# One attention and feed-forward stack on one core: the softmax steps of a unit planned closer together, its joins later, x loaded two tiles ahead, the weight check's end cut in three

## The chip, the cores and the metric

The kernel runs on one core of one Trainium2 chip. The metric is the device time of one execution in microseconds (us). Three runs of the kernel before took 2451.07, 2451.25 and 2455.77 us, so the median is 2451.25 us. One further execution was profiled. It took 2450.27 us, and its instructions span 2448.4 us of that.

Engines are named as the profile names them. PE is the matrix engine and PEld its weight load. DVE is the vector engine, ACT the scalar engine, POOL the general-purpose engine. SP has no arithmetic here and issues transfers. A trailing q (SPq, ACTq) marks the part of an engine that issues and waits. Each engine takes its instructions strictly in the order in which the program lists them for it.

## What is computed

Inputs are float32; x has 64 batches of 64 rows and 1024 columns. Cut to what matters:

```python
def reference(x, cond, lang, ...):
    y = einsum('bct,bcd->bdt', x, weights[cond])        # one 64x64 matrix chosen per batch
    qkv = y @ qkvw + qkvb                               # 32 heads of 32
    probs = softmax((q @ k.T) / sqrt(32))               # 64 x 64 per batch and head
    x = x + (probs @ v) @ ow + ob
    base = x @ W.T                                      # plus a low-rank part that top-2 gates mix
    z = base + 2.0 * lora(x, gates(x, lang))
    q, s = dynamic_quant(z * inv)                       # rounded to -127..127
    inter = clip(silu(q_g @ w_gate.T * ...) * (q_u @ w_up.T * ...), -10, 10)
    return x + dynamic_quant(inter * inv_inter) @ w_down.T * ...
```

## The kernel before

The 4096 rows are cut into 8 blocks of 512 (a block has four tiles of 128 rows, PB = 4). The first stage (function `attention`) makes queries, keys, values, softmax and context. The second makes the output projection (`OutProjection`) and the feed-forward part. Large products are done as seven smaller ones (the table `Winograd.ORDER` is 1, 6, 7, 5, 2, 4, 3); four of the operand quarters' sums are made beforehand.

**The order is written out by a planner.** `attention` is one Python loop that emits instructions for all engines. It keeps a plan time `now` and a heap `due`. `at(time, f)` puts a step into the heap. `run` (line 674) first emits every step whose time has come, then one PE product (a "fill"), then the evacuation ("rest") of the product before it, and moves `now` on by the fill's cost: 1.72 for a query or key product, 3.43 for a value product or an output product. So plan times are not waited for on the chip. They only decide the order of the instructions on each engine, and each engine then runs as fast as its order and its waits let it.

A block has four phases c = 0 to 3, one for each pair of head groups. A phase's fills are the products for the next phase: 7 for q and 7 for k, about 24 us; in phases 0 and 3 there are 7 for v as well, about 48 us. In every phase `group` emits the scores of one pair of head groups (128 small matmuls into the four PSUM banks of the pool `ps_s`, which has one buffer) and handles four units, n = 0 to 3, each 128 x 512 probabilities:

- `exponents` (L559, L560 on DVE, L564 on ACT): maximum, difference, exponential;
- `normalize` (L570 to L572 on DVE): sum, reciprocal, product;
- `parted` (L578 on ACT): a copy `ph` that lays the two 16-bit halves of each float apart; two buffers;
- `turned` (L583 on SP): a DMA transpose of `ph` into `phT`; two buffers;
- `joined` (L590 on ACT): a copy that puts the halves together again, `pT`; four buffers.

The start of unit n is planned 2.7 us after that of unit n - 1. At plan time 13.7 of the next phase `contexts` multiplies the four `pT` with the values (L603), and ACT copies the result out (`co`, L615) and stores it. Both the results of `contexts` and those of the conditional tile (below) stand in the same single `ps_s` buffer, so the next scores or the next conditional tile waits until ACT has read it.

**Conditional tiles.** `conditional_tile` makes y for one tile: 8 small matmuls (L393) that read `x` and the gathered matrix `wg`, then two copies `yh` on ACT (L404), two DMA transposes `yhT` on SP (L412) and copies into place on POOL (L426). Right after its matmuls the next tile's rows are loaded (`load_x`, L243) into the one buffer that `x` has, and POOL gathers its `wg` (L245). Most phases have one such tile. Phase 0 of block 0 has three, at plan times 13.7, 25 and 37.

**Weights.** In block 0 the weights come from the inputs, DVE or POOL makes the sums, and POOL stores the seven quarters (L291 for q and k, L311 for v). Later blocks load them ready (L293, L297). The load of a q or k job is issued when the job two places earlier has done its last product. The load of a value quarter is issued when the product that used its buffer is done; in block 0 it waits for the store of that buffer too.

**Chores.** `halve_weights` casts the feed-forward weights to bfloat16 in 24 steps and compares. It is a generator, and the planner takes one step of it at a time (two to four in a phase). Its end finds the maximum over all comparisons: a reduction on DVE, a store of one column, a load of it as a row, and a reduction of that row (L135 to L142). `combine_quarters` follows it.

In the last phase (block 7, c = 3) the fills are the first two pairs of the output projection, 14 products of 3.43. Each pair's results are also transposed: `xh` on ACT (L1198), `xhT` on SP (L1200), `xTo` on ACT (L1209), a store on SP (L1210). Then `out_dram` is stored and the next pair's `cx` and `xo` are loaded on SP (L1250, L1179, L1185).

Of the kernel before, what the change touches and what calls it, by code (L numbers as in the profile page):

```python
# [96 lines left out]
def halve_weights(tc, st, const, dram, srcs, half, any_i):  # L97


    nc = tc.nc  # L100
    parts = []
    for nm, (src, k, n) in srcs.items():
        v = src.rearrange("(k p) n -> p k n", p=P)
        parts += [(nm, v, i, slice(c, c + 512)) for i in range(k) for c in range(0, n, 512)]
    other = const.tile([P, len(parts)], F32, tag="other", name="other")
    tiles = {}

    def load(u):
        if u < len(parts):
            _, v, i, cols = parts[u]  # L110
            tiles[u] = st.tile([P, 512], F32, tag="t", name=f"hw_{u}")
            nc.sync.dma_start(tiles[u], v[:, i, cols])

    copied = None

    def compared():
        if copied:
            u, t, b = copied
            nc.vector.tensor_tensor(t, t, b, ALU.not_equal)
            nc.vector.tensor_reduce(other[:, u:u + 1], t, AX.X, ALU.max)  # L120

    load(0)
    for u, (nm, v, i, cols) in enumerate(parts):
        yield
        compared()
        load(u + 1)
        t = tiles.pop(u)
        b = st.tile([P, 512], BF16, tag="b", name=f"hb_{u}")
        nc.gpsimd.tensor_copy(b, t)
        nc.gpsimd.dma_start(half[nm][:, i, cols], b)  # L130
        copied = (u, t, b)
    yield
    compared()
    seen = st.tile([P, 1], F32, tag="seen", name="seen")
    nc.vector.tensor_reduce(seen, other, AX.X, ALU.max)  # L135
    seen_d = dram.tile([P, 1], F32, tag="seen_d", name="seen_d")
    nc.sync.dma_start(seen_d, seen)
    row = st.tile([1, P], F32, tag="row", name="row")
    nc.sync.dma_start(row, seen_d.rearrange("p o -> o p"))
    any_f = st.tile([1, 1], F32, tag="any_f", name="any_f")  # L140
    nc.vector.tensor_reduce(any_f, row, AX.X, ALU.max)
    nc.vector.tensor_copy(any_i, any_f)  # L142
    yield
# [39 lines left out]
def attention(tc, a, x_t, ctx_d, ident, dram, ps_g, KC, PB, NBLK, NCH, HPC, H, C, chores, early, op):  # L183
# [27 lines left out]
    with ExitStack() as ctx, ExitStack() as mid:  # L211
# [25 lines left out]

        def load_x(b, j, pool_=xp, tag="x"):
            i = b * PB + j
            xt = pool_.tile([P, H], F32, tag=tag, name=f"x_{i}")  # L240
            if i == PB - 1:
                held(xt[:, 0:1], x_of[0, 0][0])
            nc.sync.dma_start(xt, x_t[i])  # L243
            wg = xp.tile([P, C], F32, tag="wg", name=f"wg_{i}", bufs=4)
            nc.gpsimd.indirect_dma_start(  # L245
                out=wg[:, :],
                out_offset=None,
                in_=cw,
                in_offset=bass.IndirectOffsetOnAxis(ap=idx[:, i:i + 1], axis=0),
            )  # L250
            x_of[b, j] = xt, wg
# [130 lines left out]
        def conditional_tile(b, j, banks=None):  # L382

            xt, wg = x_of.pop((b, j))
            Y = Ys[b]
            if banks is None:
                banks = ps_s.tile([P, 4, 512], F32, tag="s", name=f"cond_{b}_{j}")
            ps = [banks[:, 2 + hf, :] for hf in range(2)]  # L390
            for hf in range(2):
                for r in range(2):
                    nc.tensor.matmul(  # L393
                        ps[hf][halves[r ^ hf], :], wg[halves[r], :], xt[halves[r], hf * 512:(hf + 1) * 512],
                        start=True, stop=True,
                    )
            if j + 1 < PB:
                load_x(b, j + 1)
            elif b + 1 < NBLK:
                load_x(b + 1, 0)  # L400

            def parted_y(hf):
                h = w.tile([P, 2, 512], I16, tag="yh", name=f"yh_{b}_{j}_{hf}", bufs=2)
                nc.scalar.copy(h, planes(ps[hf]))  # L404
                hs[hf] = h

            hs, hTs = {}, {}

            def turned_y(hf):
                h = hs[hf]  # L410
                hT = w.tile([P, 2, 512], I16, tag="yhT", name=f"yhT_{b}_{j}_{hf}", bufs=2)
                nc.sync.dma_start(  # L412
                    hT.rearrange("p h (k q) -> p (h k) q", q=P), h.rearrange("p h t -> p (h t)"), transpose=True
                )
                hTs[hf] = hT

            def joined_y(hf):
                key = f"B{hf + 1}{j // 2 + 1}"
                if j % 2 == 0:
                    Y[key] = quarter_of(b, key)  # L420
                src = hTs[hf].rearrange("p h (k q) -> p h k q", q=P)
                for r in range(2) if hf else (slice(0, P),):
                    q = halves[r ^ hf] if hf else r
                    q = slice((j % 2) * P + q.start, (j % 2) * P + q.stop)
                    dst = Y[key].bitcast(I16).rearrange("p k (q h) -> p h k q", h=2)[:, :, :, q]
                    nc.gpsimd.tensor_copy(dst, src[:, :, :, halves[r] if hf else r])  # L426

            for time, f, hf in (
                (1.7, parted_y, 0), (3.4, parted_y, 1), (3.5, turned_y, 0), (5.1, turned_y, 1), (8.5, joined_y, 0),
                (10.2, joined_y, 1),  # L430
            ):
                at(now + time, lambda f=f, hf=hf: f(hf))
# [213 lines left out]
        def group(b, c):  # L646


            def begin():
                ps = scores(b, c)  # L650
                pTs = []
                waiting.append((b, c, pTs))
                for n in range(NU):
                    at(now + 2.7 * n, lambda n=n: first(n, ps, pTs))

            def first(n, ps, pTs):
                p = exponents(b, c, n, ps)
                at(now + 10.8, lambda: normalize(b, c, n, p))
                at(now + 13.5, lambda: second(n, p, pTs))

            def second(n, p, pTs):
                h = parted(b, c, n, p)
                at(now + 1.7, lambda: third(n, turned(b, c, n, h), pTs))

            def third(n, hT, pTs):
                at(now + 6.8, lambda: fourth(n, hT, pTs))

            def fourth(n, hT, pTs):
                pTs.append(joined(b, c, n, hT))
                if (b, c) == (NBLK - 1, NP - 1) and len(pTs) == NU:  # L670
                    at(now + 3.4, contexts)
            return begin
# [76 lines left out]
        for b in range(NBLK):  # L749
            if b == 0:  # L750
                load_x(1, 0)
            for c in range(NP):
                fills, length = [], None
                if c + 1 < NP:
                    fills += qk_fill(b, c + 1)
                    if c == 0:
                        fills[7:7] = v_fill(b, 1)
                        if b == 0:
                            for at_ in range(3, 7):
                                with_sums(fills, at_, v_raw, 1)  # L760
                        if b == 0:
                            at(now + 25, lambda: conditional_tile(1, 1))
                            at(now + 37, lambda: conditional_tile(1, 2))
                    if c + 2 == NP and b + 1 < NBLK:
                        sums_to_come = [lambda b=b, n=n: t_of(b + 1, Ys[b + 1], *T_OF[n]) for n in range(4)]
                        with_sums(fills, -2, sums_to_come, 1)
                        with_sums(fills, -1, sums_to_come, 1)
                elif b + 1 < NBLK:

                    assert len(Ys[b + 1]) == 6  # L770
                    fills += v_fill(b + 1, 0) + qk_fill(b + 1, 0)
                    with_sums(fills, 0, sums_to_come, 1)
                    with_sums(fills, 1, sums_to_come, 1)
                    B = Ys[b + 1]
                else:
                    behind.pop()()
                    mid.close()
                    op.open_rest()
                    fills += op.pair(0) + op.pair(1)
                    length = 24  # L780
                if b + 1 == NBLK and c == 1:
                    assert next(chores, None) is None
                    early.close()
                    for n, load in enumerate(op.open_weights()):
                        at(now + 5 * n, load)
                phase(b, c, fills, length or sum(f[0] for f in fills))
# [1020 lines left out]
```

## Time and profile before

| what | us |
|---|---|
| median of three runs | 2451.25 |
| the profiled execution | 2450.27 |
| its span | 2448.4 |
| PE busy in the span | 2383.1 |
| DVE / ACT / POOL busy | 1358.8 / 939.4 / 432.6 |
| PE idle in 0 to 20 (start of the kernel) | 9.15 |
| PE idle in 2400 to 2448.4 (end of the kernel) | 16.3 |
| first scores from / last context to | 69.0 / 1411.3 |
| mean granted PE clock | 0.991 |

The profile has a page (busy times, 40 slices, queues, a chain of waits, groups of instructions) and can be asked for more: who waited for whom, all instructions of a stretch in order of time (the timeline), and busy times and granted clock by stretches. In a line of the waits stand the waiting instruction, what ended its wait, the total in us, how often, and the longest. In a line of the timeline stand the start, the length, the engine, the line, the operation with output and inputs, how many were merged, and in brackets the idle time before it with what ended it.

### The profile page before, as it was taken

Reading aid. Unit: us, or ns where it says so; the run is one execution under the profiler, and the core shown is the slowest. Engines: PE = TensorE matmul, PEld = TensorE weight load, DVE = VectorE, ACT = ScalarE, POOL = GpSimd, SP = SyncE. Lnnn points to the kernel's source line nnn. Section 1 sums busy time; section 2 is a strip of 40 time slices with the busy share of each in tenths; the row PEclk is TensorE's granted clock in tenths of the full one; section 3 lists DMA queues with packets and bytes.
Section 4 is the critical chain, followed back from the end, with each engine's and each line's share of the span. In section 5 each row is a group of like instructions: output and inputs, shape, how many; then the busy total and the mean of one; then the engine's idle time right before and its main releaser. Section 6 shows DMA issues by size and latency. Waiting matters only on the chain.

```text
span 2448.4 us, 41643 instructions
## 1 busy us (share of the span) xinstructions
PE 2383.1 (97%) x17104; PEld 1631.7 (67%) x17104; DVE 1358.8 (55%) x2584; ACT 939.4 (38%) x1220; POOL 432.6 (18%) x476
## 2 busy tenths in 40 slices
PE   8899999999999999999999999999999999999997
PEld 7778888888788888878888444444454545445453
DVE  3465465474463453643644632433367777878787
ACT  1235343353353343533533544344423333333333
POOL 4121121121232232310000333433200000000000
PEclk9999999999999999999999999999999999999999
DMA  8798687796797897866757768886744443434343
GB/s 291 246 272 217 194 245 207 227 253 191 212 259 214 237 251 226 242 191 195 203 150 231 211 211 261 260 252 203 237 135 82 87 80 80 87 69 92 76 115 78
DMA packets 478729, 463.23 MB, mean 189 GB/s; under 512 B 359874, under 2 KB 414147, under 8 KB 464835
## 3 DMA queue, kind: packets, MB, share of 16 engines
q1 hardware_dynamic: 448018, 393.90, 57.7%
q0 software_dynamic: 12080, 49.82, 7.8%
q10 hardware_dynamic: 18432, 16.79, 2.4%
q8 instruction: 136, 2.23, 0.4%
q14 instruction: 63, 0.51, 0.1%
HBM read 274.02 MB, written 100.66 MB: 153 GB/s over the span
## 4 chain that ended last, share of the span: by engine, by line
PE 86%; DMA 5%; ACT 3%; SPq 2%; DVE 2%; issue 1%; ACTq 0%; DVEq 0%
PE poc L1103 4%; PE pskc L491 4%; PE pskd L491 4%; PE pod L1103 4%; PE pbc L1103 4%; PE pba L1103 4%; PE pbd L1103 4%; PE poa L1103 4%; PE pska L491 4%; PE psqa L491 4%; PE psqd L491 4%; PE psqc L491 4%; PE psva L512 3%; PE psvc L512 3%; DMA phT<-ph 3%; PE psvd L512 3%
## 5 line engine op out<-in xcount | busy, mean ns | idle before, releaser
L578 ACT COPY ph<-prob 128x1024 int16<-128x1024 int16 x128 | 133.7, 1045 | 226.3 <-DMA phT<-ph 157.4
L590 ACT COPY pT<-phT 128x1024 int16<-128x1024 int16 x128 | 168.1, 1337 | 87.4 <-DMA phT<-ph 87.2
L564 ACT ACTIVATE prob<-prob 128x512 f32<-128x512 f32 x128 | 80.4, 628 | 255.0 <-DVE prob L560 254.4
L426 POOL COPY yB<-yhT 128x512 int16<-128x512 int16 (+1 forms) x84 | 86.8, 1085 | 496.8 <-DMA yhT<-yh 481.4
L1610 POOL DMA_DIRECT2D out_dram<-y x29 | 25.0, 862 | 656.3 <-DVE y L1602 644.2
L559 DVE TENSOR_REDUCE mx<-s 128x8 f32<-128x512 f32 x128 | 87.4, 683 | 75.1 <-PE s L550 75.1
L1224 POOL TENSOR_TENSOR xo<-xo,ob 128x1024 f32<-128x1024 f32 x32 | 84.9, 2672 | 221.3 <-DMA xo<-in_x_dram 213.5
L491 PE MATMUL psqa<-yB,wq 128*128 128x256 f32 x512 | 121.3, 379 | 1.3 <-ACT psqp L461 0.7
L1198 ACT COPY xh<-xo 128x1024 int16<-128x1024 int16 x64 | 64.2, 1040 | 149.8 <-DVE xo L1243 149.3
L491 PE MATMUL pska<-yB,wk 128*128 128x256 f32 x512 | 121.1, 379 | 0.2 <-ACT pskp L461 0.2
L512 PE MATMUL psva<-wv,yB 128*128 128x256 f32 x512 | 119.3, 387 | 0.0
L1103 PE MATMUL poa<-woA,cx 128*128 128x512 f32 x256 | 115.2, 593 | 0.0
L512 PEld LDWEIGHTS psva<-wv,yB 128*128 128x128 f32 x512 | 98.6, 194 | 20.9 <-issue 5.7
L1103 PE MATMUL pba<-wtA,x1T 128*128 128x512 f32 x240 | 107.9, 592 | 0.0
L491 PEld LDWEIGHTS psqa<-yB,wq 128*128 128x128 f32 x512 | 97.0, 190 | 15.4 <-ACT psqp L461 1.5
L1209 ACT COPY xTo<-xhT 128x1024 int16<-128x1024 int16 x64 | 84.8, 1338 | 58.3 <-DMA xhT<-xh 51.6
L491 PEld LDWEIGHTS pska<-yB,wk 128*128 128x128 f32 x512 | 97.2, 190 | 13.7 <-ACT pskp L461 0.6
L615 ACT ACTIVATE co<-banks,bqkv 128x256 f32<-128x256 f32 x124 | 59.0, 475 | 121.9 <-PE banks L393 89.9
L1240 POOL TENSOR_TENSOR xo<-xo,ou 128x512 f32<-128x512 f32 x48 | 59.5, 1267 | 210.4 <-DVE ou L1237 210.4
L572 DVE TENSOR_TENSOR prob<-prob,den 128x512 f32<-128x512 f32 x128 | 93.5, 730 | 4.4
L560 DVE TENSOR_TENSOR prob<-s,mx 128x512 f32<-128x512 f32 x128 | 88.5, 691 | 6.1
L1103 PEld LDWEIGHTS poa<-woA,cx 128*128 128x128 f32 x256 | 48.6, 190 | 60.4 <-issue 60.0
(258 smaller groups left out, 4978.1 us busy)
## 6 DMA issues: line engine op xcount, KB each, us to landing
wv<-v_d SPq DMA_DIRECT2D x98, 512.0 KB, 4.9
wq<-q_d SPq DMA_DIRECT2D x28, 1792.0 KB, 7.9
wk<-k_d SPq DMA_DIRECT2D x28, 1792.0 KB, 8.6
x<-in_x_dram SPq DMA_DIRECT2D x32, 512.0 KB, 5.4
ctx_d<-co ACTq DMA_DIRECT2D x128, 128.0 KB, 4.7
cx<-ctx_d SPq DMA_DIRECT2D x16, 1024.0 KB, 6.9
xo<-in_x_dram SPq DMA_DIRECT2D x32, 512.0 KB, 5.5
xT_d<-xTo SPq DMA_DIRECT2D x64, 256.0 KB, 2.8
```

The costliest lines, as they stand in the source:

```text
L426: nc.gpsimd.tensor_copy(dst, src[:, :, :, halves[r] if hf else r])
L491: nc.tensor.matmul(ps[:, 0:HB], A[:, SLOT[A_OF[i]], k, :], B[B_OF[i]][:, k, :], start=first and k == 0, stop=k == KQ - 1, skip_group_check ...
L512: nc.tensor.matmul(ps[:, j * VC:(j + 1) * VC], B[B_OF[i]][:, k, j * P:(j + 1) * P], A[:, k, :], start=first and j == 0 and k == 0, stop=k ...
L559: nc.vector.tensor_reduce(mx, ps[:, :, n, :, :], AX.X, ALU.max)
L560: nc.vector.tensor_tensor(p.rearrange("p j h k -> p h j k"), ps[:, :, n, :, :], mx.unsqueeze(3).to_broadcast([P, HPC, 2, C]), ALU.subtract,)
L564: nc.scalar.activation(p, p, AF.Exp, scale=scale)
L572: nc.vector.tensor_tensor(p, p, den.unsqueeze(2).to_broadcast([P, n, C]), ALU.mult)
L578: nc.scalar.copy(h, planes(p.rearrange("p n k -> p (n k)")))
L590: nc.scalar.copy(planes(pT.rearrange("p a b q -> p (a b q)")), hT)
L1103: self.nc.tensor.matmul(ps, self.B[self.B_OF[i]][:, k, :], self.A[self.A_OF[i]][:, k, :], start=first and k == 0, stop=k == self.KQ - 1, s ...
L1209: nc.scalar.copy(planes(xT.rearrange("p k q -> p (k q)")), hT)
L1224: nc.gpsimd.tensor_add(s["x"][:, t, :], s["x"][:, t, :], self.ob)
```

## The change

Four constants and three small pieces of code change:

- `normalize` of a unit is planned 4.0 after its exponents (was 10.8), `parted` 5.4 after (was 13.5), `turned` still 1.7 after that, and `joined` 10.3 after the transpose (was 6.8);
- `x` has two buffers in its pool, and each conditional tile loads the tile two ahead; two tiles are loaded before phase 0 of block 0;
- `halve_weights` gives way to the planner after the store of the column and after the load of the row.

```diff
@@ halve_weights
     seen_d = dram.tile([P, 1], F32, tag="seen_d", name="seen_d")
     nc.sync.dma_start(seen_d, seen)
+    yield
     row = st.tile([1, P], F32, tag="row", name="row")
     nc.sync.dma_start(row, seen_d.rearrange("p o -> o p"))
+    yield
     any_f = st.tile([1, 1], F32, tag="any_f", name="any_f")
     nc.vector.tensor_reduce(any_f, row, AX.X, ALU.max)
@@ load_x
-            xt = pool_.tile([P, H], F32, tag=tag, name=f"x_{i}")
+            xt = pool_.tile([P, H], F32, tag=tag, name=f"x_{i}", bufs=2 if tag == "x" else None)
@@ conditional_tile
-            if j + 1 < PB:
-                load_x(b, j + 1)
-            elif b + 1 < NBLK:
-                load_x(b + 1, 0)
+            if PB * b + j + 2 < PB * NBLK:
+                load_x(*divmod(PB * b + j + 2, PB))
@@ group
             def first(n, ps, pTs):
                 p = exponents(b, c, n, ps)
-                at(now + 10.8, lambda: normalize(b, c, n, p))
-                at(now + 13.5, lambda: second(n, p, pTs))
+                at(now + 4.0, lambda: normalize(b, c, n, p))
+                at(now + 5.4, lambda: second(n, p, pTs))
...
             def third(n, hT, pTs):
-                at(now + 6.8, lambda: fourth(n, hT, pTs))
+                at(now + 10.3, lambda: fourth(n, hT, pTs))
@@ attention, the loop over blocks
             if b == 0:
                 load_x(1, 0)
+                load_x(1, 1)
```

## The prediction

> **What bounds the kernel.** I read the busy times first, then the waits of PE, then the waits of SP, then the timeline around each long wait of PE.
>
> ```profile
> PE 2383.1 (97%) x17104; PEld 1631.7 (67%) x17104; DVE 1358.8 (55%) x2584; ACT 939.4 (38%) x1220; POOL 432.6 (18%) x476
> ...
> PE pskb L491 <- ACT qT L474: 8.3, 6, 1.9
> PE banks_None_None L603 <- ACT pT L590: 7.0, 2, 6.5
> PE cond L393 <- DMA x<-in_x_dram: 6.3, 1, 6.3
> PE psvc L512 <- DVE psvu L464: 5.3, 1, 5.3
> ```
>
> PE is busy for 2383 of 2448 us, so only its idle time can be won. The start and the end of the kernel, 25 us of it, are not touched. What is left is this short list, and each edit aims at one line: the weight check at 5.3, the x loads at 6.3, the softmax plan at 8.3 and 7.0. A long wait also costs clock: the window 600 to 620 has a granted clock of 0.92, and the 16 matmuls after the wait of 5.26 took 5.65 us where such sixteen elsewhere show 3.62.
>
> ```profile
> SPq L583 <- ACT pT L590: 116.1, 25, 7.2
> ...
> SPq L297 <- DMA v_d<-wv: 10.1, 1, 10.1
> ```
>
> These two waits of SP speak against the change. The first says that a transpose already waits for a join: `phT` has two buffers, so unit 2's transpose cannot go before unit 0's join is done, and everything behind it on SP stands still. The second says that in block 0 a value load held SP for 10.1 us.
>
> I followed the planner's rule for both plans to get each engine's order. In a 24 us phase the old order is transposes 0, 1, join 0, transpose 2, 3, join 1, 2, 3. The new one is all four transposes and then four joins. SP will thus stop at transpose 2 until join 0 and at transpose 3 until join 1, in every phase.
>
> **Weight check.**
>
> ```profile
> 601.07 0.38 SPq L137 DMA_DIRECT2D seen_d<-seen  x1
> ...
> 611.14 0.29 SPq L139 DMA_DIRECT2D row<-seen_d  x1
> ...
> 613.47 0.28 DVE L141 TENSOR_REDUCE any_f<-row 1x1 f32<-1x128 f32 x1 [15.16 <-DMA row<-seen_d]
> ...
> 619.85 5.65 PE L512 MATMUL psvc<-wv,yB 128*128 128x256 f32 x16 [5.26 <-DVE psvu L464]
> ```
>
> DVE stands 15.16 us for two trips to memory in a row. SP too stands 10 us, between 601.07 and 611.14. With two more yields the row load comes some 20 plan us after the store, and the reduction one chore (3.4 plan us) after the load, which landed 2.33 us after its issue (611.14 to 613.47). So DVE waits at most about 1 us, and PE's PSUM slack covers that. Won: 5.26 + (5.65 - 3.62) = **7.3 us**. Bounds 5 to 7.3. The chores needed rise by two, which pushes `combine_quarters` back by two chores; the plan has more than ten free chores before its results are read, so that costs nothing; without them the program would not build.
>
> **Rows of x.** The wait is 6.28 us, the cold matmuls after it 1.98 against 1.09 and 5.66 against 3.62. If it simply went, 9.2 us would be won. But I ask what is late next.
>
> ```profile
> 86.16 1.06 POOL L311 DMA_DIRECT2D v_d<-wv  x2
> ...
> 93.43 0.34 SPq L297 DMA_DIRECT2D wv<-v_d  x1
> 93.89 1.18 SPq L243 DMA_DIRECT2D x<-in_x_dram  x1
> ...
> 96.42 3.05 SPq L583 DMA_TRANSPOSE phT<-ph  x1
> ...
> 102.49 1.98 PE L393 MATMUL cond<-x,wg 64*64 64x512 f32 x8 [6.28 <-DMA x<-in_x_dram]
> ...
> 104.78 1.04 ACT L578 COPY ph<-prob 128x1024 int16<-128x1024 int16 x1 [12.71 <-DMA phT<-ph]
> ```
>
> x is late because SP is held until 93.43 by the value load, which waits for the store of its buffer. x itself moves ahead of this block (to about 69), good. But the softmax steps move into it. In the new order unit 3's `parted` stands on ACT ahead of both `yh` copies of tile (1,0). It needs the `ph` buffer of unit 1, hence unit 1's transpose, and that stands on SP behind the same value load. The next conditional tile needs the PSUM buffer that the `yh` copies read. So PE waits for ACT now. The time: two normalizations (1.56 us each, 86.03 to 87.59 in the old timeline) now stand on DVE before the last sums. DVE has no gap from 73.4 to 85.3, so `k_d` and `v_d` go 3.1 us later, 89.3. The store takes 7.27 (86.16 to 93.43), so SP is free at 96.5. A value load and x go first, the transpose at 98.2. Its landing took 8.3 us in this stretch (96.42 to 104.7) and 6.3 to 6.7 a little later. I take 7: 105.2. Then `parted` 1.04 and two `yh` 1.02 each: PE resumes at **108.3 instead of 102.49, 5.8 us lost**. The wait of 0.91 at 119.60 (for a join) goes. Together **+4.9**. Bounds: -9.2 (the wait goes) and +8 (the transpose lands after 9.6, the longest of the run).
>
> The Trainium skill, page "Trainium Kernel Development and Optimization", section "Best Practices", says to double-buffer so that transfers overlap with compute; by it this edit would bring the 9.2. The row of SP at 93.43 weighs more with me: a second buffer moves one load out of a blocked queue and leaves the queue blocked.
>
> **Softmax steps, in phases 3.** The six waits of `pskb` for `qT` (8.3 us) all lie in phases 3. There the ACT copy `qT` stands behind join 2, which waits for a late transpose, held by `parted` 3 and two `phT` buffers. In the new order joins 0 to 2 come some 5 us earlier against PE, and `qT` stands ahead of join 3. Following one phase (739 to 744) row by row, join 2 ends some 2 us before `qT`'s product does. All **8.3 us** go. A wait of a context for `pT` (0.7) and one of scores for `kT` (0.9) go with the earlier steps. Sum **-9.9**, bounds -11 and -3. Cover: DVE. Four normalizations and four exponents are 11.8 us, now within some 15 plan us together with 3 to 4 us of evacuations; its order puts an evacuation at most 3 us later, where the PSUM bank is needed 5 us later.
>
> **Softmax steps, in phases 1.** Here the stopped SP matters: the load `wk` for phase 3's keys stands behind transpose 3.
>
> ```profile
> 826.42 0.34 SPq L243 DMA_DIRECT2D x<-in_x_dram  x1
> ...
> 837.86 0.55 SPq L293 DMA_DIRECT2D wk<-k_d  x1
> ...
> 850.56 1.89 PE L491 MATMUL pska<-yB,wk 128*128 128x256 f32 x8
> ```
>
> The new ACT order after the context, with durations from this stretch: `co` 826.42, `parted` 2 to 828.7, `co`, `yh`, `co` to 831.1, `parted` 3 (transpose 1 goes right behind x and lands some 5.5 later) to 833.3, `co`, `yh`, join 0 to 836.6. SP: transpose 2 to 838, two `yhT` to 840.6, transpose 3 to 841.9, two chore loads (1.46), `wk` at 843.4, 5.5 us later than now. Now it has 12.7 us until its use and takes about 8.5; then it has 7.2 and, with fewer transposes beside it, about 8. So PE waits some 0.7 us in each of blocks 1 to 5 (6 and 7 have no chore loads): **+3.5**. Bounds 0 and +20 (4 us in five phases).
>
> By the page "TensorE: Matmul & The Clock Gate", Part 1, only an idle window of about 3.4 us drops the clock, so these short waits would cost no more than themselves. The rows do not quite bear that out: after an idle time of 1.72 us at 1050.30 sixteen matmuls took 4.57. At 744.08, after 1.89, nothing slowed. I add nothing; by the first row it would be up to 1 us for each wait.
>
> **The last context.** Now transposes 2 and 3 go at 1401.21, behind `out_dram` and `xo`, and PE waits 6.45 + 0.53 us, then shows 5.89 for eight matmuls instead of 3.60. In the new order they stand ahead of these, but transpose 2 waits for join 0, which stands on ACT behind two `xh` copies that need DVE's evacuation of the sixth product (1387.5 after the shifted normalizations; now 1385.2). I get join 0 at 1391.2, `xhT` landed 1396.6, `xTo` and `xh` to 1400, join 1 1401.4, transpose 3 1401.4, the next `xhT` behind it landed 1407.8, `xTo` to 1409.2, join 3 1410.5. The context ends at 1411.1 as now, but is planned one product earlier, so one more product (3.43) is left: **+3.5**. Bounds: -9.4 (the whole wait with its cold matmuls goes) and +8.
>
> **Sum.** -7.3 + 4.9 - 9.9 + 3.5 + 3.5 = -5.3. The profiled execution took 2450.27, of which 1.9 lie around its span: **2445 us**. That execution is 1.0 under the median of the three runs. A measurement of this kernel tells about 0.2% (4.9 us) from no change, so this is only just a gain.
>
> **Rivals.** *Each wait goes as meant*: x -9.2 instead of +4.9 and the end -9.4 instead of +3.5, loads in time. For it: the waits named are exactly those of the list. Against it: the orders above. 2445 - 14.1 - 12.9 - 3.5 = 2414; with x alone 2431. Together 0.2.
> *The stopped SP queue decides*: in phase 1 transposes land later than 5.5 after x, `wk` lands 4 us late in five phases: 2445 - 3.5 + 20 = 2461, slower than before. For it: 116 us of SP waiting on joins, landings up to 9.6. Against: the median landing of 4.6. It is slower by over 4.9 from a wait of 3.0 us in each of the five, an issue 7.8 instead of 5.5 us late. Chance 0.25.
> *The close steps gain nothing*: DVE and ACT, packed, evacuate later by what the joins gain, and the 9.9 stay: 2455, a little either side of the 0.2% line at 2456.2. For it: DVE without a gap in 73 to 85. Against it: DVE 55% busy. Chance 0.15.
> My forecast has 0.4, with its own range 2439 to 2450.
>
> **Range and chances.** 2429 to 2461 leaves out most of the first rival's far case and the worst queue. Faster by over 0.2% (under 2446.3): the first rival's 0.2 and 0.25 of the forecast's 0.4, together 0.45. Within: the forecast's other 0.15 and 0.05 of the third rival, 0.2. Slower: the queue's 0.25 and the third rival's other 0.1, 0.35.
>
> **What would show it.** Right: no DVE wait at `any_f`; no wait for x at the second conditional tile but one for ACT `yh` or `parted` about as long; no `pskb` wait for `qT` in phases 3; waits of `pska` for `wk` in phase 2 of blocks 1 to 5; SP waiting longer for `pT`; a wait of some 10 us at the last context. Wrong: PE passing 102 without a wait, the last context without one, or new waits of PE for DVE.

## The result, and the profile after

The changed kernel took 2491.9 us (median of four runs, 2488.9 to 2497.7), the kernel before beside it 2451.57. The ratio is 1.0163, with a 95% interval of 1.0142 to 1.0185. It is 1.6% slower; 2445 was forecast, and 2461 was the upper end of the range. The profiled execution took 2488.9 us, and its span is 2486.7, that is 38.3 longer than before. Some lines of the changed file have other numbers: L393 is now L395, L243 is L245, L293 is L295, L139 and L141 are L140 and L143, L166 is L168; those of softmax and products are the same.

First the waits of PE in the changed kernel (waiting group, what ended the wait, us in total, times, longest):

```profile
PE banks L603 <- DVE prob L560: 16.6, 10, 5.5
PE pska L491 <- DMA wk<-k_d: 13.4, 6, 3.2
PE cond L395 <- ACT yh L404: 11.8, 1, 11.8
...
PE banks_None_None L603 <- ACT pT L590: 6.7, 1, 6.7
PE banks L395 <- issue: 6.3, 2, 5.0
...
PE pskc L491 <- DVE psku L464: 3.0, 1, 3.0
PE pskb L491 <- issue: 2.9, 1, 2.9
```

The waits for `qT` (8.3) and for `x` (6.3) are gone, as meant. Two lines are new and large: contexts that wait for DVE's `prob`, which the prediction did not have at all, and `wk` with 13.4, of which it had 3.5. The idle times of PE over 0.25 us add up to 87.7 us, before to 56.6. PE's busy time is up from 2383.1 to 2388.8 with the same 17104 matmuls, because the clock was at half speed for longer (58 us against 34 between 13 and 2420). 31.1 and 5.7 make 36.8 of the 38.3.

To see where the time is lost, I took the start of the scores in each of the 32 phases from both traces and subtracted:

| stretch | longer than before, us |
|---|---|
| up to the first scores of block 1 | +11.1 |
| phase 2 of blocks 1 to 5 (3.4, 2.6, 4.1, 6.0, 8.2) | +24.4 |
| phase 0 of block 3 (the weight check) | -3.3 |
| phase 3 of blocks 1 to 6, together | -1.1 |
| phase 2 of block 7 | +3.6 |
| phase 3 of block 7 and all that follows | +2.9 |
| all others (what is left of 38.3) | +0.7 |

**The new wait for DVE.** The timeline of DVE and of PE in the changed kernel, phase 3 of block 5 (start, length, and so on; these are two answers, one of each engine):

```profile
1071.51 0.68 DVE L559 TENSOR_REDUCE mx<-s 128x8 f32<-128x512 f32 x1
1072.22 0.69 DVE L560 TENSOR_TENSOR prob<-s,mx 128x512 f32<-128x512 f32 x1
1072.83 0.68 DVE L464 TENSOR_TENSOR psvu<-psvc,psvu 128x512 f32<-128x512 f32 x1
1073.43 0.68 DVE L570 TENSOR_REDUCE den<-prob 128x8 f32<-128x512 f32 x1
1074.14 0.20 DVE L571 RECIPROCAL den<-den 128x8 f32<-128x8 f32 x1
1074.38 0.69 DVE L572 TENSOR_TENSOR prob<-prob,den 128x512 f32<-128x512 f32 x1
1074.99 0.68 DVE L559 TENSOR_REDUCE mx<-s 128x8 f32<-128x512 f32 x1
1075.70 0.69 DVE L560 TENSOR_TENSOR prob<-s,mx 128x512 f32<-128x512 f32 x1
```

```profile
1076.54 1.62 PE L603 MATMUL banks<-pT,vals 64*32 64x64 f32 x128 [0.88 <-DVE prob L560]
1083.16 1.86 PE L395 MATMUL banks<-x,wg 64*64 64x512 f32 x5 [5.00 <-issue]
```

A normalization (L570 to L572, 1.56 us) stands between the third and the fourth unit's maximum, another one earlier. Only after the fourth unit's difference, at 1076.39, has DVE read all scores, and the one buffer of `ps_s` is free for the context. In the kernel before all normalizations came after the fourth difference, which ended at 1044.76, 1.3 us before PE came to the context (DVE, then PE, same phase):

```profile
1044.07 0.69 DVE L560 TENSOR_TENSOR prob<-s,mx 128x512 f32<-128x512 f32 x1
1046.20 1.30 DVE L526 TENSOR_TENSOR vals<-psvd,psvu 128x256 f32<-128x256 f32 x3 [1.44 <-PE psvd L512]
1047.53 0.69 DVE L570 TENSOR_REDUCE den<-prob 128x8 f32<-128x512 f32 x1
```

```profile
1046.10 1.49 PE L603 MATMUL banks<-pT,vals 64*32 64x64 f32 x128
```

The second of PE's lines in the changed kernel, a wait of 5.00 that no semaphore explains, is looked at below.

**The load of the keys' weights.** SP and PE in the changed kernel, phase 2 of block 4:

```profile
854.22 1.23 SPq L583 DMA_TRANSPOSE phT<-ph  x1
855.83 3.19 SPq L412 DMA_TRANSPOSE yhT<-yh  x2
859.14 1.27 SPq L583 DMA_TRANSPOSE phT<-ph  x1
860.46 1.35 SPq L168 DMA_DIRECT2D cq<-in_ow_dram  x2
861.91 0.56 SPq L295 DMA_DIRECT2D wk<-k_d  x1
```

```profile
869.91 2.50 PE L491 MATMUL pska<-yB,wk 128*128 128x256 f32 x5 [3.17 <-DMA wk<-k_d]
```

The order on SP is the predicted one: transpose 2, `yhT`, transpose 3, chores, `wk`. The load is issued at 861.91 and PE is ready for it at 866.74 (869.91 - 3.17), 4.8 us later. Before, the same load was issued 12.7 us ahead of its use.

**Block 0 and the weight check.** ACT in block 0 of the changed kernel, then SP and DVE at the weight check:

```profile
106.46 1.04 ACT L578 COPY ph<-prob 128x1024 int16<-128x1024 int16 x1 [14.21 <-DMA phT<-ph]
107.41 1.92 ACT L404 COPY yh<-banks 128x1024 int16<-128x1024 int16 x2
```

```profile
641.13 1.26 SPq L583 DMA_TRANSPOSE phT<-ph  x1
642.48 2.73 SPq L299 DMA_DIRECT2D wv<-v_d  x4
645.26 0.32 SPq L140 DMA_DIRECT2D row<-seen_d  x1
```

```profile
650.64 0.27 DVE L143 TENSOR_REDUCE any_f<-row 1x1 f32<-1x128 f32 x1 [9.79 <-DMA row<-seen_d]
```

`parted` of unit 3 waits 14.21 us for a transpose, the copies `yh` stand behind it, and PE goes on at 109.38. At the weight check the row is now loaded one step later, but the load stands on SP behind a transpose and four value loads, and DVE waits 9.79 us where it waited 15.16.

### The profile page after: what moved, and what is told of

Read it like the earlier page. It is cut to its first block, busy times and chain, and to the rows that moved or that the text cites. A ratio compares the mean times of both kernels' runs of the same rounds, so it can differ in the third digit from the quotient of the medians.

```text
span 2486.7 us, 41601 instructions
## 1 busy us (share of the span) xinstructions
PE 2388.8 (96%) x17104; PEld 1635.5 (66%) x17104; DVE 1342.9 (54%) x2584; ACT 937.6 (38%) x1220; POOL 421.8 (17%) x476
## 4 chain that ended last, share of the span: by engine, by line
PE 84%; DMA 7%; DVE 4%; ACT 2%; issue 1%; SPq 0%; POOL 0%; ACTq 0%; DVEq 0%; POOLq 0%
PE poa L1104 5%; PE psva L512 4%; PE pbc L1104 4%; PE poc L1104 4%; PE pod L1104 4%; PE pbd L1104 4%; PE pba L1104 4%; PE pska L491 4%; PE psqa L491 3%; PE pskc L491 3%; PE psqc L491 3%; PE psqd L491 3%; PE pskd L491 3%; PE psvc L512 3%; PE psvd L512 3%; DMA phT<-ph 3%
## 5 line engine op out<-in xcount | busy, mean ns | idle before, releaser
L590 ACT COPY pT<-phT 128x1024 int16<-128x1024 int16 x128 | 170.7, 1342 | 89.9 <-DMA phT<-ph 88.3
L426 POOL COPY yB<-yhT 128x512 int16<-128x512 int16 (+1 forms) x84 | 79.0, 987 | 606.5 <-DMA yhT<-yh 606.4
L491 PE MATMUL pska<-yB,wk 128*128 128x256 f32 x512 | 126.5, 391 | 14.5 <-DMA wk<-k_d 13.4
L572 DVE TENSOR_TENSOR prob<-prob,den 128x512 f32<-128x512 f32 x128 | 93.1, 728 | 4.4
```

Of the source, the lines that this page charges most:

```text
L491: nc.tensor.matmul(ps[:, 0:HB], A[:, SLOT[A_OF[i]], k, :], B[B_OF[i]][:, k, :], start=first and k == 0, stop=k == KQ - 1, skip_group_check ...
L572: nc.vector.tensor_tensor(p, p, den.unsqueeze(2).to_broadcast([P, n, C]), ALU.mult)
L590: nc.scalar.copy(planes(pT.rearrange("p a b q -> p (a b q)")), hT)
```

## The experiments

All are single-core runs beside runs of the kernel before on the same chip. In this table "before" and "changed" say which kernel was edited. Ratios are to the kernel before.

| run | edit | median us | ratio, 95% interval |
|---|---|---|---|
| e1_weight | before + weight check | 2447.06 | 0.9984, 0.9967 to 1.0001 |
| e2_x | before + x two ahead | 2448.4 | 0.9993, 0.9977 to 1.0009 |
| e3_steps | before + the three constants | 2494.7 | 1.0172, 1.0147 to 1.0198 |
| e4_norm | before + normalize at 4.0 | 2482.08 | 1.0108, 1.0076 to 1.0140 |
| e6_late_norm | changed, normalize 8.2, parted 9.6 | 2475.25 | 1.0092, 1.0066 to 1.0118 |
| e7_pht4 | changed, four `phT` buffers | 2451.24 | 0.9999, 0.9983 to 1.0016 |
| e8_weight_x | before + weight check + x | 2449.93 | 0.9985, 0.9974 to 0.9997 |
| e11_late_norm_pht4 | changed, both of e6 and e7 | 2435.03 | 0.9924, 0.9900 to 0.9948 |
| e9_close_short | changed, joins 6.8 | 2524.22 | 1.0275, 1.0249 to 1.0301 |
| e10_before_pht4 | before + four `phT` buffers | 2440.66 | 0.9940, 0.9922 to 0.9957 |
| e12_wx_pht4 | e8 + four `phT` buffers | 2439.33 | 0.9950, 0.9931 to 0.9968 |
| e14_last_ph4 | e11 + four `ph`, last group close | 2423.87 | 0.9881, 0.9864 to 0.9899 |
| f2_norm_pht4 | e10 + normalize at 4.0 | 2469.48 | 1.0068, 1.0047 to 1.0090 |
| f3_short_pht4 | e7, joins 6.8 | 2501.62 | 1.0205, 1.0184 to 1.0225 |

### One part of the change alone

**e1_weight** and **e2_x** are the diff's first part, and its parts on `x`, on the kernel before.

> The kernel before with the weight check's end in three steps and nothing else. In the changed kernel this block came out 3.3 us shorter, not 7.3: the row load was issued only at 645.26, behind four value loads and a transpose that had held SP, and DVE waited 9.79 us for it. Theory (the closer softmax steps hold SP and so delay the row load): with the old steps the row load is issued early, DVE's wait at any_f is under 2 us, PE's wait of 5.26 us goes, about -7 us (2444.5). Rival (four value loads ahead of the row load are enough to make it late): DVE still waits some 8 us or more and the time falls by 3 us or less (2448 to 2452).

The interval just takes in no change. The row load went out at 624.67, again behind value loads, and DVE waited 10.2 us. So the lateness of the row is not the work of the closer steps: the rival holds for the cause. PE's wait of 5.26 became two smaller ones (1.22 and 2.14).

> The kernel before with the x loads two tiles ahead and nothing else. Theory (x waits only because its load stands behind the held value load; what took its place in the changed kernel comes from the softmax steps): PE's wait of 6.28 us at the second conditional tile goes with its slow matmuls, -6 to -9 us (2442 to 2445), and no ACT yh wait of over 2 us stands there. Rival (the held SP queue decides with the old steps too): an ACT or PSUM wait of 5 us or more takes the place of x, and the time is within 2 us of before.

The rival holds for the waits; 3.1 us are a little more than its 2, inside the interval. In the trace of e2_x the second conditional tile starts at 97.25 without a wait, and one tile later, at 116.98, this stands:

```profile
PE cond L393 <- ACT yh L402: 6.4, 1, 6.4
```

The `yh` copies of the second tile come behind a `parted` that waits 14.16 us for a transpose, so a wait of the kind that the prediction saw for the new order is there in the old order too, one tile later and shorter (6.4 instead of 11.8).

**e3_steps** is the diff of `first` and `third` alone.

```diff
-                at(now + 10.8, lambda: normalize(b, c, n, p))
-                at(now + 13.5, lambda: second(n, p, pTs))
+                at(now + 4.0, lambda: normalize(b, c, n, p))
+                at(now + 5.4, lambda: second(n, p, pTs))
...
-                at(now + 6.8, lambda: fourth(n, hT, pTs))
+                at(now + 10.3, lambda: fourth(n, hT, pTs))
```

> The kernel before with the three new constants of the softmax steps alone. If the three edits simply add, and the other two are worth -3 and between 0 and -9, this is 43 to 53 us slower than before (2494 to 2505), with the waits of contexts for DVE prob (17 us), of pska for wk (13 us) and block 0 some 10 to 20 us longer. If the x loads two ahead do harm of their own together with the new steps, it is less than 40 slower (under 2491).

43 slower, with 14.3 us of contexts waiting for DVE and 15.1 for `wk`. The softmax steps make the whole loss, and the other two edits are worth a few us at best.

**e4_norm** moves only the normalizations on the kernel before.

```diff
-                at(now + 10.8, lambda: normalize(b, c, n, p))
+                at(now + 4.0, lambda: normalize(b, c, n, p))
```

> The kernel before with the normalizations moved to 4.0 behind the exponents; parted, transposes and joins stay at 13.5 and 6.8. Theory (two normalizations now stand on DVE between the exponents of one group; the one score buffer in PSUM is read out later, and the context, which takes its place, waits for DVE prob): context waits for DVE prob of 0.5 to 1.9 us in every block and 5 us or more in block 0, no waits of pska for wk, 8 to 17 us slower (2459 to 2468). Rival (all comes from the stopped SP queue and the joins): no such waits, within 3 us of before.

The waits for `prob` are there as the theory has them, 8.6 us, and the kernel lost 30 us, nearly twice the 17 that the theory allowed at most. The rest of the waits of PE in e4_norm says where:

```profile
PE banks L603 <- issue: 15.2, 4, 4.9
PE cond L393 <- DMA x<-in_x_dram: 10.2, 2, 8.0
...
PE banks L603 <- DVE prob L560: 8.6, 8, 2.2
```

"issue" means that no semaphore ended the wait. These waits are taken up with f2 below.

### The two suspects taken away from the changed kernel

**e6_late_norm** puts all four exponents of a group ahead of its first normalization again.

```diff
-                at(now + 4.0, lambda: normalize(b, c, n, p))
-                at(now + 5.4, lambda: second(n, p, pTs))
+                at(now + 8.2, lambda: normalize(b, c, n, p))
+                at(now + 9.6, lambda: second(n, p, pTs))
```

> The changed kernel with the normalizations at 8.2 and parted at 9.6 behind each exponent instead of 4.0 and 5.4 (so that all four exponents of a group go ahead of its first normalization on DVE); joins stay 10.3 behind their transposes, weight check and x loads stay changed. Theory (the score buffer, read late by DVE, is the larger part of the loss): the waits of contexts for DVE prob (16.6 us in the changed kernel) go, block 0 gets 5 us or more back, 17 to 30 us faster than the changed kernel (2462 to 2475). Rival (transposes holding SP are the larger part, and they are still four in a row): the waits of pska for wk stay near 13 us, and the time falls by less than 10 (over 2482).

16.6 us came back, just under the 17 of the theory: contexts wait for `prob` only once (2.7 us), and by the first scores of block 1 the kernel is 10.0 us ahead of the changed one. The waits for `wk` are not smaller but larger, 19.4 us, as the rival had it. The waits called issue fell by 8.0 us, and the last context waits 5.7 longer for `pT`. The edit moves `parted` by 4.2 as well, so 16.6 is the net of all this. It is one cause, and e7 tells that it is not the larger one.

**e7_pht4** gives `phT` four buffers.

```diff
-            hT = p2.tile([P, 2, 4 * P], I16, tag="phT", name=f"phT_{b}_{c}_{u}")
+            hT = p2.tile([P, 2, 4 * P], I16, tag="phT", name=f"phT_{b}_{c}_{u}", bufs=4)
```

> The changed kernel with four buffers for phT instead of two, so that no transpose waits for a join. Theory (the score buffer is the larger part): SP's waits of transposes for the joins and the bias copies ahead of them (some 440 us) go, and with them the waits of pska for wk, 13 us and the slow clock behind them; the contexts' waits for DVE prob stay; 10 to 18 us faster than the changed kernel (2474 to 2482). Rival (the stopped SP queue is nearly all of the loss): 30 us or more faster (under 2462). If the wk loads are late for another reason, nothing changes (2490).

The theory that the score buffer is the larger part falls: 40.7 us came back. The waits of PE in e7_pht4:

```profile
PE cond L395 <- ACT yh L404: 11.9, 1, 11.9
PE cond L364 <- DVE wbd L379: 9.2, 1, 9.2
PE banks L603 <- DVE prob L560: 8.6, 9, 1.9
PE banks L395 <- issue: 6.0, 2, 4.8
```

No wait for `wk` is left. The phases 2 of blocks 1 to 5 are shorter than in the changed kernel by 2.8, 2.4, 5.0, 5.9 and 8.2, together 24.3 us, which is what they had lost. Another 8.6 came after the last scores (the wait of 6.66 at the last context is gone), 3.2 in the block of the weight check. SP still stands at transposes for long, contrary to what I expected. The profile puts 195.8 us of it down to ACT's `qT`; in the rows such a transpose goes out when the `parted` just ahead of that `qT` ends (820.36 and 820.39). What counted was not how long SP stands in all but whether it stands ahead of a load that is needed: its waits at transposes are 525 us in all in the changed kernel and 308 in the kernel before, and 324 in e7_pht4, but also 296 in e6_late_norm, where `wk` is late, and 525 in e9_close_short, where PE does not wait for it.

**e11_late_norm_pht4** does both.

> The changed kernel with both: normalizations at 8.2, parted at 9.6, and four buffers for phT. If score buffer and stopped SP queue are two separate causes, the gains of the two single experiments add and the time comes to that of the kernel before or below it (2440 to 2455). If one of them only hides the other, it is no better than the better single one.

The two gains add: 2491.9 - 16.6 - 40.7 = 2434.6, measured 2435.03. They are two causes.

**e8_weight_x**, **e10_before_pht4**, **e12_wx_pht4** ask what is left of the change's own gain.

> The kernel before with the weight check in three steps and the x loads two ahead; the softmax steps are left as before. Alone they measured 4.5 and 3.1 us below before, each inside its interval. Theory (they lie in different blocks and add): 2442 to 2445, PE waiting some 6 us for ACT yh in block 0 in place of x, and 2 to 4 us at the weight check. Rival (what they won was the drift of one call of runs): within 3 us of before.

-3.1 us, between theory and rival, an interval that ends just below 1. The two do not add to the 7.6 of the single runs; with intervals of about 4 us either way that tells nothing.

> The kernel before with four phT buffers and nothing else. There too the fourth transpose of a group stands ahead of the second join, and SP waits 116 us for pT. Theory (in the kernel before these waits have cover, so the buffers are worth only the waits of pskb for qT, 8.3 us, at most): 0 to 8 us faster (2445 to 2453). Rival (SP held by transposes costs the kernel before as well): 15 us or more faster.

13 us faster, between the two. All six waits of `pskb` for `qT` are gone there without any change of the steps. So these waits, which the change went after, came from the two `phT` buffers.

> The kernel before with the weight check, the x loads and four phT buffers; the softmax steps stay as before. It tells what the steps are worth once the buffers no longer stop SP: with late normalizations, close parted and long joins that kernel measured 2435. Theory (the six waits for qT and the early joins are worth some 8 us): 2440 to 2447 here. Rival (the buffers alone make the 2435, the steps nothing): 2432 to 2438.

2439.33 lies between the two again, 4.3 us above e11, and its interval overlaps that of e11 (0.9931 to 0.9968 and 0.9900 to 0.9948). Whether the closer steps are worth anything once the buffers are there, these runs do not tell.

### Shorter joins, and a faster kernel

**e9_close_short** and **f3_short_pht4** put the joins back to 6.8 in the changed kernel, with two and with four `phT` buffers.

> The changed kernel with the joins 6.8 behind their transposes instead of 10.3; two phT buffers, normalizations at 4.0. With four buffers the changed kernel came to 2451. Theory (what holds SP is the time from the third transpose of a group to the first join, 4.9 plan us with 10.3 and 1.4 with 6.8): most of the 40 us of the four buffers come back without them, 2455 to 2470, and the waits of pska for wk fall from 13.4 to under 5 us; the waits for DVE prob stay. Rival (the earlier steps hold SP, however long the joins take): over 2480.

The waits for `wk` are gone, as the theory said, but the kernel lost another 32 us. That is over the 2480 of the rival, though not for its reason, since PE waits for no `wk`. ACT in e9_close_short:

```profile
391.74 1.34 ACT L590 COPY pT<-phT 128x1024 int16<-128x1024 int16 x1 [0.95 <-DMA phT<-ph]
396.84 1.34 ACT L590 COPY pT<-phT 128x1024 int16<-128x1024 int16 x1 [3.76 <-DMA phT<-ph]
398.04 0.62 ACT L564 ACTIVATE prob<-prob 128x512 f32<-128x512 f32 x1
398.57 0.57 ACT L461 COPY psvp<-psva 128x512 f32<-128x512 f32 x1
```

Two joins wait for a transpose to land, and the exponentials of the next group and the evacuation `psvp` stand behind them. DVE then waits 3.09 us for `psvp` at 399.17, its last difference ends at 407.55, and the context waits 5.05. Contexts wait 29.0 us for `prob` in this kernel. So with the early steps the longer join was the useful part of the edit.

> The changed kernel with four phT buffers and joins 6.8 behind their transposes (2451 with 10.3). With two buffers the short joins cost 32 us over the changed kernel, and ACT stood 127 us at joins for a transpose to land. Theory (ACT waits at a join for the landing, and exponents and evacuations queue behind it, whatever the buffers): with four buffers still 10 us or more slower than 2451 (over 2461), ACT's wait for phT over 100 us. Rival (the landings were late only because SP was held by the two buffers): within 5 us of 2451.

50 us slower than e7_pht4 without the ring of two, so with the early steps shorter joins cost time whatever the buffers, as the theory said. ACT's wait for `phT` at the joins is 84.4 us, though, not over 100, against 15.3 in e7_pht4. The kernel before has 87.2 and the changed one 88.3 of these waits, so their sum does not tell the cost; it hangs on what stands behind the joins.

**f2_norm_pht4** is the edit of e4_norm with four buffers.

> The kernel before with four phT buffers and the normalizations at 4.0 (parted 13.5, joins 6.8). With the buffers alone it measured 2440.7; with two buffers the early normalizations cost 30 us, though taking them back out of the changed kernel won only 16.6. Theory (their cost is that of the score buffer and does not hang on the phT buffers): 2455 to 2462 here, waits of contexts for DVE prob of some 9 us. Rival (with two buffers the late exponents also made transposes and joins late, and that was the other half): under 2452. If instruction fetch is the other half, the fetch gaps of PE stay near 25 us and the time is 2465 or more.

29 us over e10_before_pht4, the same as with two buffers: the cost of early normalizations does not hang on the ring. The waits for `prob` are 9.5 us, those called issue 22.6; in e10 they are none and 6.3 (without PE's first wait). So more of the cost stands in the second kind than at the score buffer, and of the expectation it is the last sentence that the numbers fit. PE in f2_norm_pht4, and the instruction queue among the transfers of 553 to 560 (packets, MB, share of the 16 engines):

```profile
553.09 1.21 PE L603 MATMUL banks<-pT,vals 64*32 64x64 f32 x103 [1.78 <-DVE prob L560]
557.80 0.66 PE L603 MATMUL banks<-pT,vals 64*32 64x64 f32 x25 [3.50 <-issue]
```

```profile
q8 instruction: 2, 0.03, 2.1%
```

PE stops after 103 of 128 small matmuls, at 554.30. A 16 KB packet of the instruction queue starts at 555.4 and takes 0.93 us, and PE goes on at 557.80. Every wait of this kind over 2 us behind the start of the kernel, in all the traces of this study, has such a packet: it starts between 0.6 us before and 4.1 us after PE stops and ends 0.8 to 1.5 us before PE goes on. I read these waits as instruction fetch from that; the profile does not name it. In f2 four of the five longest at contexts and conditional tiles come right behind a wait for `prob`, in e4 two of five.

**e14_last_ph4** goes after what e11 still showed, 10.93 us in block 0 and 7.34 at the last context.

```diff
         def group(b, c):
+            t_n, t_p = (4.0, 5.4) if (b, c) == (NBLK - 1, NP - 1) else (8.2, 9.6)
...
-                at(now + 8.2, lambda: normalize(b, c, n, p))
-                at(now + 9.6, lambda: second(n, p, pTs))
+                at(now + t_n, lambda: normalize(b, c, n, p))
+                at(now + t_p, lambda: second(n, p, pTs))
...
-            h = p2.tile([P, 2, 2 * HPC * C], I16, tag="ph", name=f"ph_{b}_{c}_{u}")
+            h = p2.tile([P, 2, 2 * HPC * C], I16, tag="ph", name=f"ph_{b}_{c}_{u}", bufs=4)
```

> The kernel of 2435 (late normalizations, four phT buffers) with four ph buffers as well, and in the very last group the normalizations at 4.0 and parted at 5.4. What is left there: 10.93 us in block 0 for ACT yh, which stands behind a parted that waits for a ph buffer, and 7.34 us at the last context. Theory (both go, the last one as in the changed kernel with four buffers): PE waits under 5 us in block 0, none at the last context, 10 to 18 us faster (2417 to 2425). Rival (in block 0 the value load that holds SP makes the next one late, so yhT or a join takes the place): block 0 keeps 5 us or more, 2425 to 2432.

11.2 us faster than e11, and faster than both kernels: 0.9881 of the kernel before, 0.9864 to 0.9899. The waits of PE in e14_last_ph4:

```profile
PE banks L603 <- DVE prob L560: 4.9, 2, 4.0
PE cond L395 <- ACT yh L404: 3.5, 1, 3.5
PE banks L395 <- issue: 2.0, 1, 2.0
```

In block 0 the second tile no longer waits. The third waits 3.5 us, for `yh` copies that wait for a `yhT` to land, and two more waits follow there, 1.9 for `yh` and 4.0 for `prob`. The last context waits 0.82.

## Why the prediction was wrong

Two steps failed. The working of DVE's order left out the score buffer, which had no term. The term for the late `wk` was much too small, and it is the larger part of the miss.

**Softmax steps, in phases 3: a step that left out a wait.** -9.9 was forecast, -1.1 came (one of the six waits lay in block 0). The waits for `qT` did go, all of them. But the step "Cover: DVE" looked only at the evacuations that stand behind the normalizations, and not at the scores themselves. DVE's four differences are also what frees the only score buffer, and the next user of it, the context, comes 12 plan us after the scores. Two normalizations of 1.56 us ahead of the fourth difference were enough. The contexts wait 6.1 us for it in phases 3 of blocks 1 to 6, and the 5.00 called issue at 1083 follows one of these waits. In block 0 they wait 8.6 us. e6_late_norm shows what the order costs (16.6 us net), and e4 and f2, which move the normalizations alone, cost 29 to 30 us, of which the waits for `prob` themselves are only 8.6 and 9.5.

**Softmax steps, in phases 1: the mechanism right, the term mis-sized.** The wait for `wk` is the predicted one at the predicted place (the scores of phase 2 are its border), +3.5 forecast, +24.4 measured. The load took 7.5 to 8.0 us from its issue to its use, as said. But PE was ready 4.8 to 5.6 us after the issue, not 7.2: the waits were 2.02, 1.91, 3.19, 3.17 and 2.42, not 0.7 each. Most of the rest of the 24.4 is what follows a wait: 17.1 us of half clock in blocks 3 to 5, about 8.5 of time, where the prediction said "I add nothing", and one wait of 2.10 called issue. This is the rival *the stopped SP queue decides*, which named the point from which it decides (a load 7.8 us late); against PE it was 7.0 to 8.3 us late. e7_pht4 shows it, since the same 24.3 came back. What was not tried is the `wk` load alone on another queue.

**Rows of x.** PE was said to resume at 108.3 behind ACT's `yh` and resumed at 109.38: right. The +4.9 of this step is +5.7 at the next scores. With the old steps (e2_x) a wait of 6.4 us of this kind stands one tile later, so not all of it is the steps' work. The rest of block 0's +11.1 lies in phases 1 to 3, where the contexts wait 8.6 us; with late normalizations (e6) block 0 is only 1.1 us longer than before.

**Weight check.** -7.3 forecast, -3.3 measured. The step "landed 2.33 us after its issue" was taken from a load with nothing on SP in the 9 us ahead of it: here issue to landing took 5.4 us, and the issue itself stood behind four value loads, 4.4 us after DVE had come to the reduction. The sentence "PE's PSUM slack covers that" was made for a wait of 1 us; the wait was 9.79.

**The last context.** +3.5 forecast, +2.9 measured. The context comes one product earlier, as the working said, and PE waits 6.66 there; of the "some 10 us" the rest went to a wait for `prob` at 1410.40 (1.92, and a slow clock behind it), which was not foreseen.

**The sum.** Measured against forecast: weight check +4.0, block 0 +6.2, phases 3 +8.8, phases 2 +20.9, last context -0.6, phase 2 of block 7 +3.6 (a wait of 2.86 called issue and 0.65 of `wk`), others +0.7. That is 43.6, the distance from -5.3 to +38.3. The range held the rival's 20 us but not the score buffer beside it, which had no term.

**Open.** Why PE's fetch comes late in kernels with early normalizations is not settled. The waits called issue make 10.6 to 25.3 us in the seven kernels that normalize all groups at 4.0, and 4.2 to 9.1 in the nine others (without PE's first wait). That a context which had to wait runs through its small matmuls faster than its instructions come in would fit the place of some of these waits (four of the five in f2, two of the five in e4); no run takes the fetch apart from the wait.

## What to carry to other kernels

When a step is moved earlier on an engine, list what that engine still has to read to free a buffer, and for each single buffer ask who takes it next; covering the evacuations is not enough. A transfer that waits for a buffer stands in front of everything behind it on its queue, so before steps are moved to shorten such a wait, try more buffers: here four instead of two for `phT` took away the six waits for `qT` that the steps were moved for, without moving a step. In the changed order a copy that finishes a transfer belonged late on its engine: put earlier, it stopped what stood behind it until the landing.

## What the runs showed of the hardware

**The clock fell after idle times shorter than 3.4 us.** PE in the changed kernel:

```profile
1039.61 3.62 PE L491 MATMUL pska<-yB,wk 128*128 128x256 f32 x8 [2.42 <-DMA wk<-k_d]
```

Eight such matmuls took 1.89 us elsewhere; behind an idle time of 2.42 us the granted clock was at half for 3.41 us. After 3.19 and 3.17 us it fell too (3.41 and 6.83 us of half clock); so did it after 2.10 us at 1046.71 and 1.92 us at 1410.40 (3.41 each). After 2.02 and 1.91 us in blocks 1 and 2 it did not, so the length of the idle time alone does not tell. The Trainium skill, page "TensorE: Matmul & The Clock Gate", Part 1, puts the drop behind one idle window of about 3.4 us; the 2.42 us here speaks against reading that as a lower bound for a gap.

**Instruction fetch was not hidden.** The Trainium skill, page "Runtime: NRT & Kernel Launch", section "Instruction fetch mechanics", says that each engine fetches its next 16 KiB block by itself while it runs, mostly hidden. The packets of 16,384 bytes agree with that. But PE stood still for 7.9 us of waits called issue before, 12.3 in the changed kernel and 25.3 in e4_norm, mostly in runs of 128 small matmuls or right behind them, and a single one took 5.00 us with a packet of 0.92.
